# A routed expert layer on one core: accumulated rows fetched two steps earlier, with more row buffers and a smaller descriptor memory for GpSimd's transfers

## The chip, the cores and the metric

The kernel runs on one core of a Trainium2 chip. The core has five engines with instruction queues of their own: TensorE (PE in the profile; its weight loads are listed as PEld), VectorE (DVE), ScalarE (ACT), GpSimd (POOL) and SyncE (SP), and 16 DMA engines that move data. The metric is the device time of one execution in microseconds, lower is better. The kernel before takes 320.92 us, the median of three runs (320.69 to 323.11).

## The reference

The input x is 8 × 256 tokens of 512 numbers in f32. Two gated blocks follow one another, each added to its own input:

```python
x = x + jnp.tanh(g_xattn[0]) * _L0_xattn_ref(_layernorm(x), ctx_2048, mask_BxS2_bk0)
x = x + jnp.tanh(g_ffn[0]) * _L0_ffn_ref(_layernorm(x), w_router, w_gate, w_up, w_down)

# attention: few of the 256 context rows of each batch are unmasked
scores = einsum('bsd,bmd->bsm', h, ctx) / sqrt(512)
out = einsum('bsm,bmd->bsd', softmax(where(mask, scores, -1e30)), ctx)

# experts: 8 of them, inner width 192, each token uses its best 2
probs = softmax(xt @ w_router.T)
top_v, top_i = top_k(probs, 2); top_v = top_v / sum(top_v)
out = einsum('tei,ehi,te->th', silu(g) * u, w_down, comb)
```

g and u are the token's products with the expert's w_gate and w_up; comb holds the two weights of a token at its two experts. What matters here is the second block: 2048 tokens, each computed by two experts, the two results added.

## The kernel before

**First stage (to about 99 us).** Attention runs over 16 tiles of 128 tokens. It also works out each token's two experts and sorts the tokens into lists per expert, one set of lists for first choices and one for second choices. Each list is padded to tiles of 128 rows, so a tile belongs to one expert. The centred tokens, with their scales and weights behind them, are written to a table xc_d in the chip's main memory (rows of 576 numbers); ids holds, per tile, which row each of its 128 places takes. A padded place has the number of an extra row. In this stage the row buffers (tag "row", 512 numbers in each of 128 partitions) hold centred contexts, squares (L398) and the one-hot rows at_row and at_col (L440) that build the tables.

**Expert stage.** The function run (L700) goes through 38 tiles: 19 of first choices, then 19 of second choices. A tile takes these functions:

- gather (L632): GpSimd's indirect transfer fetches 128 rows by ids. With "xg" it reads xc_d into one of eight places in xall (the ring); with "acc" it reads acc_d into a row buffer.
- turn (L648): PE transposes the tile (pt_g), ACT copies it out (xT_g).
- gate_up (L651): PE multiplies with the expert's gate and up weights (pgu), ACT and DVE form h.
- flip (L669): PE transposes h (pht), DVE copies it (hT).
- down (L678): PE multiplies with the down weights (py), ACT scales the result into a row buffer y (L686). For a first-choice tile DVE adds the token's residual (L688) and GpSimd scatters y to acc_d (L645). For a second-choice tile y waits.
- add (L693): a second-choice tile's y gets the accumulated rows acc added on DVE (L695) and GpSimd scatters it to the output (L645).

Each scatter is followed on GpSimd by a one-element memset (spacer, L461). The scatters to one table are declared independent of one another; a gather from acc_d depends on all scatters to it.

**What sets the order.** The whole stage is inside a manual schedule: every engine executes its instructions in the order in which the code issues them. At step s, run issues in turn: xg for tile s + 4 (AHEAD), gate_up of tile s, flip of s - 1, turn of s + 2, down of s - 2, then acc for tile s - 3 and add for tile s - LAG = s - 4, the last two for second-choice tiles alone. There are 38 + LAG steps. Behind the down of tile 18, the last first-choice tile (step 20), a branch (L726, L728) goes round extra tiles, which this input does not need; the same branch closes the stage. GpSimd's indirect transfers thus stand in one queue: xg, acc and out of each step, in that order.

Row buffers come in a ring of 7, shared by y and acc; a buffer is written again once its last reader is done. The memory in which GpSimd writes the descriptors of its transfers lies in the core's working memory too; the program's call at L769 names no size for it, which gives 16384 bytes per partition.

Of the kernel before, what the change touches and what calls it, by code (L numbers as in the profile page):

```python
# [31 lines left out]
Q2 = NQ  # L32
# [14 lines left out]
def gated_xattn_moe(ctx: ExitStack, tc: tile.TileContext, x, xT, ctxn, ctxT, mask, maskT, g_x, g_f, wr, wgu, wd, out):  # L47
    nc = tc.nc
# [4 lines left out]
    wk = ctx.enter_context(tc.tile_pool(name="work", bufs=1))  # L53
# [7 lines left out]
    def make(pool, size, tag, bufs, shape, name):  # L61
        if not apart:
            return pool.tile(shape, FP, tag=tag, bufs=bufs, name=name)
        key = "bank" if tag == "ps" else name.split("_")[0]
        if key not in apart[0]:
            apart[0][key] = pool.tile([P, size], FP, tag=tag, bufs=bufs, name=name)
        n = math.prod(shape[1:])
        v = apart[0][key][0:shape[0], 0:n]
        return v if len(shape) == 2 else v.rearrange("p (a b) -> p a b", a=shape[1])

    def row(shape, name):
        return make(wk, 512, "row", 7, shape, name)

    def half(shape, name):
        return make(wk, 256, "half", 8, shape, name)
# [68 lines left out]
    acc_d = dr.tile([T + 1, D], FP, name="acc_d")  # L144
# [112 lines left out]
    def m_centre(p):  # L257

        g = row([P, D], f"cc_{p}")
        nc.scalar.activation(g, cns[p], AF.Identity, bias=KEEP["cmv", p][:, 0:1], scale=-1.0)  # L260
        KEEP["cc", p] = g
# [21 lines left out]
    def long_way():  # L283
# [8 lines left out]
        for b in range(B):  # L292
# [7 lines left out]
            for i in range(b * TT, (b + 1) * TT):  # L300
                nc.vector.bn_stats(one["l_st"], xs[i])
                nc.vector.bn_aggr(mv, one["l_st"])
                nc.vector.tensor_scalar(mv[:, 1:2], mv[:, 1:2], EPS, None, ALU.add)
                nc.gpsimd.tensor_tensor(rs, mv[:, 1:2], expo, ALU.pow)
                xa = row([P, D], "lx")
                nc.vector.tensor_scalar(xa, xs[i], mv[:, 0:1], rs, ALU.subtract, ALU.mult)
                xaT = turned(xa, "l")
# [15 lines left out]
                for c in range(MC):  # L323
                    nc.tensor.matmul(pav, lhsT=prT[:, c, :], rhs=cn[:, c, :], start=(c == 0), stop=(c == MC - 1))
                more = row([P, D], "lm")
                nc.vector.tensor_scalar(more, pav, den, None, ALU.mult)
                nc.vector.tensor_add(xs[i], xs[i], more)
# [367 lines left out]
        nc.vector.tensor_add(y, y, a)  # L695
        scatter(out, q, y, "out")

    AHEAD, LAG = 4, 4

    def run(qs, side=None, after=None):  # L700

        n = len(qs)

        def at(f, s, *more):
            if 0 <= s < n:
                f(*more[:1], qs[s], *more[1:]) if more else f(qs[s])
        for s in range(min(AHEAD, n)):
            at(gather, s, xc_d, "xg")
        for s in range(min(2, n)):
            at(turn, s)  # L710
        for s in range(n + LAG):
            at(gather, s + AHEAD, xc_d, "xg")
            at(gate_up, s)
            at(flip, s - 1)
            at(turn, s + 2)
            at(down, s - 2)
            if side and s >= 2 and s - 2 < n and qs[s - 2] == after:
                side()
            if 0 <= s - 3 < n and qs[s - 3] >= Q2:
                at(gather, s - 3, acc_d, "acc")  # L720
            if 0 <= s - LAG < n and qs[s - LAG] >= Q2:
                at(add, s - LAG)

# [18 lines left out]
    with tc.manual_schedule(engines={PE, DVE, ACT, POOL, SP}):  # L742
        run([*range(N0), *range(Q2, Q2 + N0)], lambda: more_tiles(0), N0 - 1)
        more_tiles(1)
# [31 lines left out]
```

## Time and profile before

| | us |
|---|---|
| median of three runs | 320.92 |
| the profiled execution | 320.94 |
| its span, first to last instruction | 319.2 |
| PE busy | 261.9 (82%) |
| POOL busy | 150.8 (47%) |
| DVE busy | 131.7 (41%) |
| ACT busy | 115.4 (36%) |
| POOL, xg gathers (38) | 37.0 busy, 975 ns each; 3.5 us to landing |
| POOL, acc gathers (19) | 18.2 busy, 957 ns each; 3.6 us to landing |
| POOL, scatters to acc_d (19) | 19.3 busy, 1015 ns each; 2.8 us to landing |
| POOL, scatters to out (19) | 19.3 busy, 1015 ns each; 2.8 us to landing |
| DVE, adds of acc (19) | 12.9 busy, 680 ns each |

The profile is of one execution. Busy time counts an engine's instructions; the time of an indirect transfer on POOL is the time that GpSimd is occupied with it, while its data land later, and the landing is counted from the issue. A line of the profile's order of time has the start, the length, the engine, the source line, the operation with output and inputs, and in brackets how long the engine was idle before it and what ended that. The mean granted clock of PE is 0.944 of full speed.

### The profile page before, as it was taken

The numbers are of one execution on the slowest core, as the hardware profiler recorded it, in microseconds if no ns is written. First come the engines' busy times: TensorE is split into PE (matmuls) and PEld (weight loads), VectorE is DVE, ScalarE is ACT, GpSimd is POOL, SyncE is SP. The second block draws the span as 40 slices with busy tenths as digits, with TensorE's granted clock in tenths as the row PEclk, the third lists the DMA queues.
The fourth block names the chain that finished last, engine by engine and source line by source line (L and its number), as shares of the span: only waits on it lengthen the run. The fifth ranks groups of instructions, "written<-read, shape, count | busy, mean of one in ns | idle before, by whom it ended". The sixth has DMA issues, their size and how long they took to land. (4 is left out here: it accounts for less than half of the span.)

```text
span 319.2 us, 4026 instructions
## 1 busy us (share of the span) xinstructions
PE 261.9 (82%) x1100; PEld 165.7 (52%) x1100; DVE 131.7 (41%) x449; ACT 115.4 (36%) x275; POOL 150.8 (47%) x238
## 2 busy tenths in 40 slices
PE   3377897979850999999999999989999999999100
PEld 3265676767630566555555565545556555555000
DVE  3329988886760024333443334422242332425100
ACT  1123677767640233333332333323233332422100
POOL 4328855665654404253353443524656566444610
PEclk9999999999975699999999999999999999999855
DMA  5699769697214602233323324316355554423510
GB/s 165 222 349 310 249 231 341 221 367 280 94 75 130 203 3 90 88 106 105 113 93 109 103 99 137 105 57 177 129 150 160 166 173 148 139 76 100 161 61 0
DMA packets 16077, 48.55 MB, mean 152 GB/s; under 512 B 3181, under 2 KB 3181, under 8 KB 16048
## 3 DMA queue, kind: packets, MB, share of 16 engines
q0 software_dynamic: 7984, 25.64, 25.7%
q1 hardware_dynamic: 5888, 17.85, 16.3%
q10 hardware_dynamic: 2176, 4.72, 3.8%
q8 instruction: 13, 0.21, 0.3%
q14 instruction: 16, 0.13, 0.1%
HBM read 35.08 MB, written 14.68 MB: 156 GB/s over the span
## 5 line engine op out<-in xcount | busy, mean ns | idle before, releaser
L658 PE MATMUL pgu<-wgu_sb,xT_g 128*128 x304 | 106.1, 492 | 0.9 <-ACTq L728 0.9
L658 PEld LDWEIGHTS pgu<-wgu_sb,xT_g 128*128 128x128 f32 x304 | 58.1, 192 | 49.4 <-issue 17.9
L682 PE MATMUL py<-wd_sb,hT 96*128 x152 | 71.4, 592 | 0.0
L664 DVE SCALAR_TENSOR_TENSOR th<-th,pgu 128x192 f32<-128x192 f32 x38 | 13.5, 354 | 103.0 <-ACT th L663 103.0
L645 POOL DMA_INDIRECT acc_d<-y,ids x19 | 19.3, 1015 | 60.3 <-DVE y L688 57.6
L640 POOL DMA_INDIRECT xall<-xc_d,ids x38 | 37.0, 975 | 17.9 <-DMA xc_d<-xr 5.0
L663 ACT ACTIVATE th<-pgu,xall 128x192 f32<-128x192 f32 x38 | 16.0, 421 | 75.2 <-PE pgu L658 75.2
L686 ACT ACTIVATE y<-py,xall 128x512 f32<-128x512 f32 x38 | 26.1, 687 | 42.1 <-PE py L682 40.0
L682 PEld LDWEIGHTS py<-wd_sb,hT 96*128 96x128 f32 x152 | 25.9, 190 | 18.8 <-issue 18.8
L445 POOL TENSOR_SCALAR ac<-cols,low,idt 128x128 f32<-128x128 f32 x32 | 27.5, 869 | 14.8 <-DVE low L439 13.8
L645 POOL DMA_INDIRECT out<-y,ids x19 | 19.3, 1015 | 31.6 <-DVE y L695 29.3
L181 PE MATMUL pt_g<-ident,xall 128*128 128x128 f32 x152 | 23.8, 281 | 8.8 <-issue 8.3
L183 ACT COPY xT_g<-pt_g 128x512 f32<-128x512 f32 x38 | 22.3, 586 | 19.6 <-PE pt_g L181 19.6
L688 DVE SCALAR_TENSOR_TENSOR y<-xall,y 128x512 f32<-128x512 f32 x19 | 14.3, 752 | 28.7 <-ACT y L686 28.7
L181 PEld LDWEIGHTS pt_g<-ident,xall 128*128 128x128 f32 x152 | 18.3, 144 | 9.6 <-issue 8.5
L354 PE MATMUL psc<-cT,xT 128*128 128x137 f32 x128 | 19.1, 293 | 3.9 <-ACT cT L268 3.2
L640 POOL DMA_INDIRECT acc<-acc_d,ids x19 | 18.2, 957 | 5.4 <-issue 5.4
L354 PEld LDWEIGHTS psc<-cT,xT 128*128 128x128 f32 x128 | 17.0, 199 | 5.0 <-ACT cT L268 3.9
L384 PE MATMUL pav<-cn,prT 128*128 128x512 f32 x32 | 16.4, 594 | 0.0
L695 DVE TENSOR_TENSOR y<-y,acc 128x512 f32<-128x512 f32 x19 | 12.9, 680 | 8.4 <-DMA acc<-acc_d,ids 8.2
L666 DVE SCALAR_TENSOR_TENSOR h<-th,xall,pgu 128x192 f32<-128x192 f32 x38 | 15.8, 415 | 1.4
L673 PEld LDWEIGHTS pht<-ident,h 128*96 128x96 f32 x76 | 9.6, 126 | 12.7 <-issue 7.5
(149 smaller groups left out, 294.7 us busy)
## 6 DMA issues: line engine op xcount, KB each, us to landing
wgu_sb<-wgu SPq DMA_DIRECT2D x8, 768.0 KB, 7.9
xc_d<-xr ACTq DMA_DIRECT2D x8, 576.0 KB, 4.0
xT<-xT SPq DMA_DIRECT2D x8, 512.0 KB, 5.0
wd_sb<-wd SPq DMA_DIRECT2D x8, 384.0 KB, 7.1
xall<-x SPq DMA_DIRECT2D x1, 2048.0 KB, 13.3
xall<-x SPq DMA_DIRECT2D x2, 512.0 KB, 4.1
xall<-x SPq DMA_DIRECT2D x1, 1024.0 KB, 9.2
xall<-xc_d,ids POOLq DMA_INDIRECT x38, 3.5
```

Of the source, the lines that this page charges most:

```text
L181: nc.tensor.transpose(pt[:, c, :], src[:, c * P:(c + 1) * P], ident)
L183: nc.scalar.copy(dst, pt)
L354: nc.tensor.matmul(both, lhsT=xTs[b][:, c, t * P:(t + 1) * P], rhs=cTs[p % 2][:, c, :], start=(c == 0), stop=(c == HC - 1))
L384: nc.tensor.matmul(pav, lhsT=prT, rhs=cns[p], start=True, stop=True)
L445: nc.gpsimd.tensor_scalar(at_col[:, n, :], cols, low[:, n:n + 1], idt[:, i:i + 1], ALU.is_equal, ALU.mult)
L640: nc.gpsimd.indirect_dma_start(out=g, out_offset=None, in_=src[:, :], in_offset=bass.IndirectOffsetOnAxis(ap=ids[:, q:q + 1], axis=0))
L645: free(nc.gpsimd.indirect_dma_start(out=dst, out_offset=bass.IndirectOffsetOnAxis(ap=ids[:, q:q + 1], axis=0), in_=z, in_offset=None, boun ...
L658: nc.tensor.matmul(pgu, lhsT=xgT[:, c, :], rhs=wgu_sb[:, bass.ds(v * GU + c * 2 * I, 2 * I)], start=(c == 0), stop=(c == HC - 1))
L663: nc.scalar.activation(th, pgu[:, 0:I], AF.Tanh, scale=xg[:, RS:RS + 1])
L666: nc.vector.scalar_tensor_tensor(h, th, xg[:, R2:R2 + 1], pgu[:, I:2 * I], ALU.mult, ALU.mult)
L682: nc.tensor.matmul(py, lhsT=hT[:, k, :], rhs=wd_sb[:, bass.ds(v * DN + k * D, D)], start=(k == 0), stop=(k == 1))
L686: nc.scalar.activation(y, py, AF.Copy, scale=xg[:, c:c + 1])
```

## The change

The order in run is changed: acc is gathered for tile s - 1 at step s instead of tile s - 3, and the add comes at step s for tile s - 3 instead of s - 4 (LAG 3), so that there are 41 steps instead of 42. The row buffers become 12 instead of 7. The descriptor memory of GpSimd's transfers becomes 2048 bytes per partition instead of 16384.

```diff
     def row(shape, name):
-        return make(wk, 512, "row", 7, shape, name)
+        return make(wk, 512, "row", 12, shape, name)
...
-    AHEAD, LAG = 4, 4
+    AHEAD, LAG = 4, 3
...
-            if 0 <= s - 3 < n and qs[s - 3] >= Q2:
-                at(gather, s - 3, acc_d, "acc")
+            if 0 <= s - 1 < n and qs[s - 1] >= Q2:
+                at(gather, s - 1, acc_d, "acc")
             if 0 <= s - LAG < n and qs[s - LAG] >= Q2:
                 at(add, s - LAG)
...
-    nc = bacc.Bacc("TRN2", target_bir_lowering=False, num_devices=1)
+    nc = bacc.Bacc("TRN2", target_bir_lowering=False, num_devices=1, dynamic_dma_scratch_size=2048)
```

In the compiled order of the instructions, GpSimd's queue behind the branch was xg 25, xg 26, acc 19, xg 27, acc 20, out 19; it is now acc 19, xg 25, acc 20, xg 26, acc 21, out 19. At the end its last six transfers were out 34, acc 36, out 35, acc 37, out 36, out 37; they are now acc 36, out 34, acc 37, out 35, out 36, out 37. DVE's adds each stand one step earlier; PE's order is the same.

## The prediction

> **What bounds the kernel now.** I read the busy times over the span first, then busy time by stretches, then the chain of waits, and last the order of time at the end and between the two passes.
>
> ```profile
> PE   3377897979850999999999999989999999999100
> ...
> PEclk9999999999975699999999999999999999999855
> ...
> POOL acc L640 5%; POOL out L645 4%; POOL xall L640 3%; PE pgu L658 2%; PE py L682 1%; POOL spacer L461 1%; PE pt_g L181 0%; ACT xT_g L183 0%; PE pht L673 0%; POOLq L726 0%; POOLq L645 0%; POOLq L640 0%; ACTq L183 0%
> ```
>
> One slice is 8 us. From 136 to 296 us PE is full; its last three slices are empty. The chain of what ended last nevertheless runs through POOL's acc, out and xall transfers. Both can hold at once: POOL's last piece is the end of the kernel, while PE sets the pace before it. The stretches settle which:
>
> ```profile
> 225.00:287.00 62.00, 62.00 (x226) 35.91 (x225) 20.59 (x49) 20.76 (x37) 35.42 (x49) 1.00 0.48 146
> 287.00:306.00 19.00, 9.39 (x27) 4.30 (x25) 6.32 (x13) 3.17 (x5) 10.34 (x16) 0.85 0.39 127
> 306.00:319.00 13.00, 0.00 (x0) 0.00 (x0) 0.00 (x0) 0.00 (x0) 0.00 (x0) 0.50 0.04 16
> ```
>
> Columns: length, then PE, weight load, DVE, ACT, POOL. In the second pass PE is busy 62.00 of 62.00 us at clock 1.00: there, POOL's waits cost nothing. In the 19 us after it PE works 9.39 us, and this stretch is where an earlier gather can pay. Its POOL and DVE instructions, in order of time (start, length, releaser):
>
> ```profile
> 290.10 0.97 POOL L640 DMA_INDIRECT acc<-acc_d,ids  x1 [0.25 <-issue]
> ...
> 293.30 1.01 POOL L645 DMA_INDIRECT out<-y,ids  x1 [2.23 <-DVE y L695]
> ...
> 294.62 0.97 POOL L640 DMA_INDIRECT acc<-acc_d,ids  x1 [0.25 <-issue]
> ...
> 295.90 1.02 POOL L645 DMA_INDIRECT out<-y,ids  x1 [0.30 <-issue]
> 296.43 0.69 ACT L686 ACTIVATE y<-py,xall 128x512 f32<-128x512 f32 x1 [1.03 <-PE py L682]
> ...
> 297.22 0.98 POOL L640 DMA_INDIRECT acc<-acc_d,ids  x1 [0.24 <-issue]
> 298.12 0.69 DVE L695 TENSOR_TENSOR y<-y,acc 128x512 f32<-128x512 f32 x1 [3.89 <-DMA acc<-acc_d,ids]
> ...
> 300.41 0.98 POOL L640 DMA_INDIRECT acc<-acc_d,ids  x1 [0.25 <-issue]
> ...
> 303.86 0.69 DVE L695 TENSOR_TENSOR y<-y,acc 128x512 f32<-128x512 f32 x1 [2.43 <-DMA acc<-acc_d,ids]
> 304.83 1.02 POOL L645 DMA_INDIRECT out<-y,ids  x1 [2.04 <-DVEq L728]
> ```
>
> Count the tiles of both passes 0 to 37, steps likewise. The last y (tile 37) is ready at 296.43 + 0.69 = 297.12, but its accumulated rows are asked for at 300.41, since that gather stands in step 40, behind four acc and out transfers. They land 3.45 us later, the add runs at 303.86, and the last out is issued at 304.83. So 7.7 us pass from a ready y to the last scatter, nearly all of it queue order.
>
> **acc gathered two steps earlier, add one step earlier.** The rows give the new order in the tail. Tile 35's gather takes the place of tile 33's in step 36, before this fence; tile 36's takes 290.10, tile 37's takes 294.62. DVE's adds each move up one place, into slots where the trace already has an add of the same length (step 37: 292.34; step 38: 293.54). So the out transfers at 293.30 and 295.90 keep their times and now carry tiles 34 and 35. Tile 36: y ready 295.40, add to 296.14, out behind POOL's previous transfer and spacer at 297.22. Tile 37: gather 294.62 + 3.45 = 298.1 (y is ready at 297.12), add 0.69 us to 298.8, out 0.28 us later at 299.07. Before: 304.83. Gain 304.83 - 299.07 = 5.76 us. The late one is now the landing of tile 37's gather, 1.0 us behind its y. The 13.3 us from the last spacer (305.91) to the end hold the last landing (2.2 to 4.2 us, median 2.8) and the program's close, which are unchanged and move along.
>
> Bounds: tile 37's out cannot precede 298.55 (POOL free behind tile 36's out and spacer), a gain of 6.3 us; with the longest landing of such a gather (4.9 us) it is 1.45 us later, a gain of 4.3 us.
>
> **Between the passes.** The first acc gather moves from third to first in POOL's queue behind the branch (step 20), and must wait for the last acc_d scatter.
>
> ```profile
> 209.94 1.01 POOL L645 DMA_INDIRECT acc_d<-y,ids  x1 [2.66 <-DVEq L728]
> ...
> 214.62 0.97 POOL L640 DMA_INDIRECT xall<-xc_d,ids  x1 [3.60 <-DMA acc_d<-y,ids]
> ...
> 215.89 0.95 POOL L640 DMA_INDIRECT xall<-xc_d,ids  x1 [0.30 <-issue]
> ```
>
> POOL waits for that landing already, in front of a gather that does not read acc_d: the branch's not-taken side waits for all of POOL's transfers. So the new wait is old. Queued behind the acc gather, tile 25's xg goes from 214.62 to about 215.9 and lands at 219.4; PE turns that tile at 221.9. Tile 26's goes from 215.89 to 218.4, lands at 221.9, is turned at 226.86. Cost nothing; were the first cover gone, at most the 1.27 us between two POOL transfers. Tile 19's add stands at 218.5, its rows land at 214.62 + 3.6 = 218.2.
>
> **Second pass, steady.** Each step still issues one xall, one acc and one out, and the out still waits for an add at the same place in DVE's queue. The xall at 225.67 lands 3.5 us later and is first read by PE's transposes at 236.77, so PE's 4.96 us a step stay. Cost nothing; the cover is those 7.6 us between landing and transposes.
>
> **12 row buffers.** Two rows a step in the second pass mean that a buffer comes round after six steps. Its last reader is then done for at least two steps, so no gather waits for a buffer. In the first stage the buffers carry at_row, at_col and squares; two of the eight groups of at_col instructions lose a wait on PE. The last of them (89.27) starts 0.19 us behind DVE's low (89.08), its ordinary handoff, so 0; a bound of 1.0 us gain is POOL's whole idle time put down to PE there.
>
> **Descriptor memory an eighth as large.** No row shows its filling. The trace has POOL transfers starting 1.28 us apart at the closest and gathers landing within 4.9 us: four open at once. If the chip must check an older transfer before it reuses memory, that costs δ per transfer; a gain is excluded, since the same rows are described. Bounds: 0, and 1.0 us (a transfer's whole busy time on POOL, 0.96 to 1.02). Nearest row: POOL's queue takes a semaphore event in 17 to 43 ns, so I take 0.04. Three transfers lie on the tail's path (out, acc, out): 0.1 us. By the Trainium skill (DMA: Bandwidth & Descriptors, sections Terms and The descriptor swizzle) a 128-partition transfer writes 9 descriptors of 16 bytes per engine and side, by which, as an estimate, 2048 bytes hold 128, or 14 transfers: no waiting for room; no trace here shows the filling.
>
> **Sum.** 5.76 - 0.1 = 5.7 us. The profiled run took 320.94 us (span 319.2), 0.02 above the median 320.92: 315.2 us.
>
> **Rivals.**
> Slower: δ is large. In the second pass POOL's step is 0.975 + 0.957 + 1.015 + 0.09 busy and about 0.80 of handoffs, 3.84 of 4.96 us; room 1.12 us, or 0.37 per transfer (first pass: two transfers, room 1.2 per transfer). Steps 22 to 33 issue three each: backlog 12 × (3δ - 1.12). Steps 34 to 37 issue two and win back 4 × (2.27 - 2δ), as a step of about 4.85 us holds 2.58 + 2δ. The tail adds 3δ. At δ = 1: 22.6 - 1.1 + 3 - 5.76, so +18.7 or 340 us. The gain is gone at δ = 0.6; over 0.67 it is over 1% slower. For it: wrapping has no row. Against: it needs ten times the nearest row. Chance 0.11.
>
> Serial transfers: the memory holds so little that each transfer waits for the one before to land. A first-pass step takes 2.8 + 3.5 = 6.3 us for 4.96, a second-pass one 3.5 + 3.6 + 2.8 = 9.9 us: 19 × 1.3 + 15 × 4.9 = 98, about 415 us. The Trainium skill (Perfetto Trace Analysis, DMA Instruction — SWDGE) says that the engines start early "particularly if more descriptors are generated than fit in the descriptor buffer"; by that rule a full buffer holds up GpSimd, which the trace with the large memory cannot show. Against: five gathers in a row are held to nothing but 1.28 us each, and an eighth would have to be less than two transfers. Chance 0.06.
>
> No gain: the acc gathers are earlier in the queue but the tail's end stays, by δ between 0.5 and 0.67, or because tile 37's rows land 5 us late among the outs. 318 to 324, likeliest 320.9. Against: 3.4 us landings in that same traffic. Chance 0.11.
>
> **Numbers.** Within 1% (3.2 us) this kernel can't be told from no change. Forecast 315.2, chance 0.72; its own range 313.6 (gain 6.3 and the 1.0 us of at_col) to 317.5 (landing +1.45, δ up to 0.3). To leave out under 2 in 10 the range takes in the no-gain case: 313.6 to 321.0. Faster by over 1% 0.72, same 0.11, slower 0.17.
>
> **What would show it.** Right: the last out is issued about 8.3 us, not 14.0, after the last gate-and-up matmuls end (290.80); its add released by y's or acc's landing within 1 us of the last y; PE still full to 296. Wrong: POOL's indirect transfers longer than 1.0 us or more than 0.3 us apart where nothing is waited for (δ); out waits growing step by step through the second pass; PE idle before pt_g; a tail whose adds still wait over 2 us for acc.

## The result and the profile after

The changed kernel takes 307.03 us, the median of four runs (306.57 to 308.71). The kernel before takes 321.29 us (four runs, 320.69 to 323.11). The ratio is 0.9565, with a 95% interval of 0.9517 to 0.9613. That is 14.3 us less, where 5.7 were predicted; 307.03 lies 6.6 us below the bottom of the predicted range.

The profiled execution of the changed kernel took 308.71 us, the slowest of the four, with a span of 307.0 us. Cut at three events which both profiles have, the two spans compare like this (us; "gate-up" is the pgu matmuls of L658):

| part of the span | before | after | difference |
|---|---|---|---|
| start to the first xg gather | 99.63 | 101.84 | +2.2 |
| to the end of the last gate-up | 191.17 | 191.32 | +0.1 |
| to the issue of the last out | 14.03 | 8.83 | −5.2 |
| to the end of the span | 14.38 | 5.00 | −9.4 |
| span | 319.21 | 306.98 | −12.2 |

The first row varies between executions: the change leaves that stage's order alone but for two buffer waits, and a second profile of the same changed kernel (e7 below) has 99.94 there. Why it varies was not found: four of the six profiles of the changed order with a small memory have 101.5 to 101.8, every other profile of the whole kernel 99.6 to 100.1. Without this row the profiles differ by 5.2 + 9.4 = 14.6 us, close to the 14.3 us of the medians. The third row is what was predicted. The fourth is not: it was taken as unchanged.

The busy time over the span and the chain of waits, from the page of the changed kernel:

```profile
PE   3289798888964199999999999998999999999990
...
PEclk9999999999996579999999999999999999999997
...
PE 24%; issue 3%; POOL 3%; DVE 1%; POOLq 0%; ACT 0%
PE pgu L658 13%; PE py L682 8%; PE pt_g L181 2%; POOL out L645 1%; PE pht L673 1%; POOL acc L640 1%; DVE y L695 0%; ACT th L663 0%; DVE h L666 0%; POOL spacer L461 0%; DVE th L664 0%; DVE hT L675 0%; POOLq L726 0%; POOLq L645 0%
```

One slice is 7.7 us. PE now has one empty slice at the end, where it had two and one nearly empty. The chain, which ran back through POOL's acc, out and xall transfers before, now runs through POOL for the last transfers only and then through PE's gate, up and down products: with the last gathers out of the way, PE's work is what leads to the end. The stretches of the changed kernel (length; then busy time and count of PE, weight load, DVE, ACT, POOL; then clock, DMA share, GB/s):

```profile
225.00:287.00 62.00, 62.00 (x224) 35.70 (x223) 21.75 (x52) 21.50 (x38) 35.65 (x49) 1.00 0.51 153
...
303.00:307.00 4.00, 0.00 (x0) 0.00 (x0) 0.00 (x0) 0.00 (x0) 0.04 (x1) 0.50 0.13 51
```

In the second pass PE is as full as before, 62.00 of 62.00 us at clock 1.00. The empty stretch behind the last instruction, 13 us before, is 4 us. DMA is busy 13% of those 4 us against 4% of the 13: the same last landing in a shorter time.

The tail in order of time, where the last gate-up ends at 290.40 + 2.75 = 293.15:

```profile
290.40 2.75 PE L658 MATMUL pgu<-wgu_sb,xT_g 128*128 x8
...
295.65 1.01 POOL L645 DMA_INDIRECT out<-y,ids  x1 [2.22 <-DVE y L695]
...
296.97 0.98 POOL L640 DMA_INDIRECT acc<-acc_d,ids  x1 [0.24 <-issue]
...
297.78 0.69 DVE L695 TENSOR_TENSOR y<-y,acc 128x512 f32<-128x512 f32 x1 [1.25 <-ACT y L686]
298.25 1.12 POOL L645 DMA_INDIRECT out<-y,ids  x1 [0.30 <-issue]
298.78 0.69 ACT L686 ACTIVATE y<-py,xall 128x512 f32<-128x512 f32 x1 [1.03 <-PE py L682]
...
299.67 1.02 POOL L645 DMA_INDIRECT out<-y,ids  x1 [0.24 <-issue]
...
301.01 0.69 DVE L695 TENSOR_TENSOR y<-y,acc 128x512 f32<-128x512 f32 x1 [2.54 <-DMA out<-y,ids]
301.98 0.99 POOL L645 DMA_INDIRECT out<-y,ids  x1 [1.24 <-DVE y L695]
302.95 0.09 POOL L461 MEMSET spacer<- 1x1 f32 x1
```

Tile 37's gather starts 3.82 us behind the last gate-up and its y is ready at 298.78 + 0.69, 6.32 us behind it: both to the hundredth where the prediction put them (294.62 and 297.12 against 290.80). From the gather's issue to the add that needs its rows it is 301.01 − 296.97 = 4.04 us instead of the 3.45 assumed, so the last out is issued 8.83 us behind the last gate-up, not 8.27. The view puts that wait down to an out transfer; by the trace's landing records the gather landed at 300.93, 0.08 us ahead of the add, and the out then under way (298.25) only at 301.78, so it was the rows. The tile before it no longer waits for rows: its add at 297.78 is released by y itself.

What fills the last stretch is not in any view, since semaphore and drain instructions are not counted as busy. They are in the trace's records, though. GpSimd's own, with start in us and length in ns (one of each in the first 0.6 us is left out):

```
before   11.77   198 semaphore | 212.65  1167 semaphore | 307.84  2177 semaphore
        310.05  8324 drain     | 318.59   107 drain     | 318.94    40 drain
after    11.77   197 semaphore | 215.00   447 semaphore | 304.96   337 semaphore
        305.33   811 drain     | 306.36   107 drain     | 306.70    40 drain
```

"Semaphore" is the instruction that the records name INC_SWDGE_SEM. It stands at a branch of the first stage, when GpSimd has made one transfer, at the branch between the passes, and at the close of the program, where a drain follows. Before, the last out (304.83) had landed when this instruction began at 307.84; then the two instructions took 2.18 + 8.32 = 10.5 us. After, they take 0.34 + 0.81 = 1.15 us. The difference, 9.35 us, is the whole of the fourth row.

### The profile page after: what moved, and what is told of

It reads as the page before. It is cut to its first block, busy times and chain, and to the rows that moved or that the text cites. A ratio compares the mean times of both kernels' runs of the same rounds, so it can differ in the third digit from the quotient of the medians.

```text
span 307.0 us, 4001 instructions
## 1 busy us (share of the span) xinstructions
PE 265.1 (86%) x1100; PEld 168.5 (55%) x1100; DVE 131.6 (43%) x449; ACT 115.4 (38%) x275; POOL 151.1 (49%) x238
## 5 line engine op out<-in xcount | busy, mean ns | idle before, releaser
L658 PE MATMUL pgu<-wgu_sb,xT_g 128*128 x304 | 106.2, 492 | 0.9 <-ACTq L728 0.9
L658 PEld LDWEIGHTS pgu<-wgu_sb,xT_g 128*128 128x128 f32 x304 | 58.2, 193 | 49.4 <-issue 17.9
L640 POOL DMA_INDIRECT xall<-xc_d,ids x38 | 37.1, 976 | 14.6 <-issue 6.1
L688 DVE SCALAR_TENSOR_TENSOR y<-xall,y 128x512 f32<-128x512 f32 x19 | 14.3, 751 | 28.7 <-ACT y L686 28.7
L354 PE MATMUL psc<-cT,xT 128*128 128x137 f32 x128 | 20.0, 303 | 3.9 <-ACT cT L268 3.2
L354 PEld LDWEIGHTS psc<-cT,xT 128*128 128x128 f32 x128 | 18.0, 209 | 5.2 <-ACT cT L268 3.9
L384 PE MATMUL pav<-cn,prT 128*128 128x512 f32 x32 | 17.3, 623 | 0.0
L675 DVE COPY hT<-pht 96x256 f32<-96x256 f32 x38 | 15.7, 414 | 0.0
```

The costliest lines, as they stand in the source:

```text
L354: nc.tensor.matmul(both, lhsT=xTs[b][:, c, t * P:(t + 1) * P], rhs=cTs[p % 2][:, c, :], start=(c == 0), stop=(c == HC - 1))
L384: nc.tensor.matmul(pav, lhsT=prT, rhs=cns[p], start=True, stop=True)
L640: nc.gpsimd.indirect_dma_start(out=g, out_offset=None, in_=src[:, :], in_offset=bass.IndirectOffsetOnAxis(ap=ids[:, q:q + 1], axis=0))
L658: nc.tensor.matmul(pgu, lhsT=xgT[:, c, :], rhs=wgu_sb[:, bass.ds(v * GU + c * 2 * I, 2 * I)], start=(c == 0), stop=(c == HC - 1))
```

## The experiments

Theory A, formed on these records: the close costs a fixed time for each transfer that the descriptor memory still holds. GpSimd has made 101 transfers at the end; by the theory 16384 bytes hold them all, 2048 only the latest few. The semaphore instruction gives a first slope: 198 ns with 1 transfer made, 1167 with 50 at the branch, 2177 with 101, so (1167 − 198) / 49 and (2177 − 1167) / 51, both 20 ns each. The drain would be 8324 / 101 = 82 ns each. The rivals are that the order, or the buffers, shortened the end and the memory nothing, or that the cost goes with the size of the memory, whatever it holds.

### One part at a time

**e1**, the memory alone, is the kernel before with

```diff
-    nc = bacc.Bacc("TRN2", target_bir_lowering=False, num_devices=1)
+    nc = bacc.Bacc("TRN2", target_bir_lowering=False, num_devices=1, dynamic_dma_scratch_size=2048)
```

> The kernel before with the descriptor memory at 2048 bytes and nothing else. Theory A (the close of the program grows with what the descriptor memory holds): GpSimd's last drain falls from 8.3 to about 0.8 us and the semaphore instruction ahead of it from 2.2 to 0.3 us, so the last out to the end of the span takes about 5.0 us instead of 14.4, and the time is 321.3 - 9.4 = about 312; the tail of out and acc transfers keeps its 14.0 us from the end of the last gate-and-up matmuls to the last out. Rival B (the close is shorter because the order of the last transfers changed): 321, with 14.4 us behind the last out. Rival C (the smaller memory also speeds or slows transfers in the middle): the stretch from the first xg gather to PE's end differs from 196.8 us by over 1 us.

**e2**, the order alone, is the changed kernel with the large memory; 12 row buffers don't fit beside it, so it has 7:

```diff
-        return make(wk, 512, "row", 12, shape, name)
+        return make(wk, 512, "row", 7, shape, name)
...
-    nc = bacc.Bacc("TRN2", target_bir_lowering=False, num_devices=1, dynamic_dma_scratch_size=2048)
+    nc = bacc.Bacc("TRN2", target_bir_lowering=False, num_devices=1)
```

> The changed order (acc for tile s - 1, add for s - 3) with 7 row buffers and 16384 bytes of descriptor memory, as 12 buffers do not fit beside it. Theory A: only the tail gets shorter, 14.0 to 8.8 us from the end of the last gate-and-up matmuls to the last out, the end behind it stays 14.4 us: 321.3 - 5.2 = about 316. Rival B: the close falls to 5 us, about 307. If the buffers are needed: acc gathers or y wait for a buffer and the gain is under 4 us.

**e3** is the changed kernel with 7 row buffers (the first of these two edits alone).

> The changed kernel with 7 row buffers instead of 12. If the buffers carry nothing: 307.0 within 1 us, the same tail of 8.8 us. If they are what lets the gathers run early: out of acc gathers that wait for a buffer, a longer tail, up to 312.

**e4** is the kernel before with half the memory, `dynamic_dma_scratch_size=8192`.

> The kernel before with 8192 bytes of descriptor memory. Theory A by what is held: the memory holds some 56 of the 101 transfers (each taking 9 of 512 places), at 82 ns each in the drain (8324 ns over 101) and 20 ns in the semaphore instruction: drain 4.6 us, semaphore instruction 1.3 us, time 321.3 - 4.6 = 316.7. Theory A by size alone: half of 8.3 and 2.2 us, time 316.1. Rival B: 321.

All four were timed beside the kernel before (median 321.24, seven runs). The last two columns are from their profiles.

| kernel | median, us | ratio (95%) | last gate-up to last out | last out to end |
|---|---|---|---|---|
| before | 321.24 | | 14.03 | 14.38 |
| e1, memory alone | 311.77 | 0.9696 (0.9646 to 0.9747) | 13.74 | 5.09 |
| e2, order alone | 316.19 | 0.9821 (0.9768 to 0.9874) | 9.14 | 14.35 |
| e3, changed, 7 buffers | 307.43 | 0.9545 (0.9491 to 0.9599) | 9.12 | 5.02 |
| e4, half the memory | 315.33 | 0.9804 (0.9751 to 0.9857) | 13.76 | 9.20 |

The two parts are separate and add up: 9.5 us for the memory and 5.05 for the order make 14.5, where 14.3 were to be explained. The tails of e1 and e2, in order of time, show each with one half of the change:

```profile
300.69 0.98 POOL L640 DMA_INDIRECT acc<-acc_d,ids  x1 [0.24 <-issue]
...
303.98 0.69 DVE L695 TENSOR_TENSOR y<-y,acc 128x512 f32<-128x512 f32 x1 [1.91 <-DMA acc<-acc_d,ids]
304.95 1.02 POOL L645 DMA_INDIRECT out<-y,ids  x1 [1.21 <-DVE y L695]
...
305.94 0.09 POOL L461 MEMSET spacer<- 1x1 f32 x1
```

This is e1: the last add still waits for acc, and the last out starts at 304.95, as before (304.83). From the first xg gather to the last gate-up e1 takes 191.34 us, where before has 191.17, so the small memory doesn't slow the transfers in the middle. In its stretches (the same columns as above) the end that follows is as short as in the changed kernel:

```profile
306.00:310.00 4.00, 0.00 (x0) 0.00 (x0) 0.00 (x0) 0.00 (x0) 0.03 (x1) 0.50 0.13 51
```

And e2, its tail and then its stretches:

```profile
295.33 0.97 POOL L640 DMA_INDIRECT acc<-acc_d,ids  x1 [0.25 <-issue]
...
299.67 0.69 DVE L695 TENSOR_TENSOR y<-y,acc 128x512 f32<-128x512 f32 x1 [2.84 <-DMA acc<-acc_d,ids]
300.64 0.99 POOL L645 DMA_INDIRECT out<-y,ids  x1 [1.54 <-DVE y L695]
301.61 0.09 POOL L461 MEMSET spacer<- 1x1 f32 x1
```

```profile
302.00:315.00 13.00, 0.00 (x0) 0.00 (x0) 0.00 (x0) 0.00 (x0) 0.00 (x0) 0.50 0.04 16
```

Its acc comes early and its last out starts at 300.64, but the 13 empty us stand behind it as before. The records of GpSimd's closing instructions follow the memory and not the order (ns):

```
              memory   semaphore   drain
before, e2     16384  2177, 2182    8324
e4              8192        1162    4159
after, e1, e3   2048    337, 342     811
```

e4 tells a size between the two ends. Its closing semaphore instruction, 1162 ns, is as long as the one with 50 transfers made at the branch (1167), so by the theory about 50 were still held. Its drain then costs 4159 / 50 = 83 ns each; a line through the two drains gives (8324 − 4159) / 51 = 82 ns each and some 0.1 us besides. The semaphore instruction of 337 ns after the change means about 8 held, by which the drain would be 0.7 us; it is 0.81. By size alone e4 would show half of 2177 and 8324 ns, and it does, so e4 doesn't decide between the two rules (and its median, 315.33, lies about 1 us below what was expected by either); the one length of 1167 ns at the branch with 16384 bytes speaks for the transfers, and the small kernels below decide it. The Trainium skill (DMA: Bandwidth & Descriptors, the section on the descriptor swizzle) counts nine descriptors per engine and side for a transfer of 1 MiB to 128 partitions; with 16 bytes for each (its section Terms) 56 transfers fit in 8192 bytes and 14 in 2048, as an estimate. The counts of about 50 and 8 that the lengths tell agree with that: they lie below those bounds. By the theory the older ones were cleared away in passing.

e3 answers for the buffers. In e3's profile, the acc gathers (count, then lowest, median and longest ns, and when), and below them the idle time in front of all 57 gathers of that line, xg and acc, and what ended it (us and count):

```profile
L640 POOL DMA_INDIRECT acc<-acc_d,ids x19: 942/946/1764, 216.2 to 296.6; - x19
...
  issue: 14.4, 42
  DMA xc_d<-xr: 5.0, 1
  ACT th L663: 3.5, 14
```

No wait for a reader of a row buffer is among them with 7, and its time, 307.43, is that of the changed kernel. The 12 buffers carry nothing.

### The cost by itself

Does the close go by the transfers held or by the bytes? And what does it cost to reuse a small memory while work goes on? Four small kernels make GpSimd gather 128 rows of x in a loop, with 8 buffers, and store the first 16:

```python
for i in range(GATHERS):
    k = i % NT
    g = wk.tile([P, D], FP, tag="g", name=f"g_{i}")
    nc.gpsimd.indirect_dma_start(out=g, out_offset=None, in_=x[:, :],
                                 in_offset=bass.IndirectOffsetOnAxis(ap=ids[:, k:k + 1], axis=0))
    if i < NT:
        nc.sync.dma_start(out=out[k * P:(k + 1) * P, :], in_=g)
```

m1 has 32 gathers and 16384 bytes, m2 96 and 16384, m3 96 and 2048, m4 32 and 32768.

> A small kernel alone: 32 gathers of 128 rows of x by GpSimd, the first 16 stored to the output; attention and experts are left out. Descriptor memory 16384 bytes. If the drain grows with the transfers that were made and not yet cleared away (82 ns each): 32 x 82 = 2.6 us. If it grows with the size of the memory: 8.3 us as in the kernel before.

> The same with 96 gathers in 16384 bytes. By transfers: 96 x 82 = 7.9 us. By size: 8.3 us, the same as with 32 gathers.

> 96 gathers in 2048 bytes, of which the memory holds 14 at a time. By transfers held: at most 14 x 82 = 1.1 us. By size: 1.0 us. Clearing transfers away in between should show in the gathers: none over 1.2 us and a spacing as with 16384 bytes if it is cheap, 0.1 us more a gather if it costs what the drain costs.

> 32 gathers in 32768 bytes. By transfers: 2.6 us as with 16384 bytes. By size: 16.6 us.

| | time, us | span | start of the last gather | from there to the end |
|---|---|---|---|---|
| m1, 32 of 16384 | 51.21 | 49.1 | 43.37 | 5.69 |
| m4, 32 of 32768 | 51.01 | 48.9 | 43.32 | 5.54 |
| m2, 96 of 16384 | 135.77 | 134.0 | 124.36 | 9.64 |
| m3, 96 of 2048 | 130.60 | 128.8 | 123.88 | 4.95 |

m1 and m4 agree to 0.15 us with memories of different size, and neither shows the 8.3 or 16.6 us that the size alone would give, so the bytes don't count. 64 more gathers in the same memory make the close 3.95 us longer (m2 against m1), and with the small memory those 96 close within 4.95 us. In m2 the drain ends 7.9 us after GpSimd has issued its last gather: 96 × 82 ns. One expectation can't be read as it was put: the 2.6 us for 32 transfers do not show in m1. There the last gather takes 3.56 us to land and the drain ends 1.35 us behind the landing, less than 2.6, so part of its work seems to lie beside the landing. All these transfers are of 128 rows: whether the close goes by the transfer or by its descriptors is not shown. The numbers are of one execution each.

In m2 and m3 the gathers themselves (line; busy time in us and mean ns; idle time before them and what ended it), and their last:

```profile
L27 POOL DMA_INDIRECT g<-x,ids x96 | 90.8, 946 | 33.5 <-issue 26.5 <-DMA out<-g 6.4 <-DVE ids L23 0.6
...
124.36 0.95 POOL L27 DMA_INDIRECT g<-x,ids  x1 [0.30 <-issue]
```

```profile
L27 POOL DMA_INDIRECT g<-x,ids x96 | 90.9, 947 | 33.0 <-issue 29.1 <-DMA out<-g 2.5 <-DMA g<-x,ids 0.8
...
123.88 0.95 POOL L27 DMA_INDIRECT g<-x,ids  x1 [0.30 <-issue]
```

946 and 947 ns each, 0.30 us apart, and the last one at the same time to 0.5 us, although the small memory is written over many times: clearing in passing costs nothing that can be seen. Together with e1 this settles the prediction's δ, and its rival of serial transfers too. The Trainium skill (Perfetto Trace Analysis, DMA Instruction — SWDGE) speaks of more descriptors than fit in the buffer; with 2048 bytes no gather in m3 was held up by it. With 1024, in e6 and e8 below, a few single transfers took 1.2 to 1.7 us, as single ones did with more memory.

### What is late next

In the changed kernel tile 37's add waits 1.5 us for its rows (y at 299.47, add at 301.01). **e5** asks for them one step earlier still, and two tiles at the first step behind the branch:

```diff
-            if 0 <= s - 1 < n and qs[s - 1] >= Q2:
-                at(gather, s - 1, acc_d, "acc")
+            for i in (s - 1, s) if s == N0 + 1 else (s,) if s > N0 + 1 else ():
+                at(gather, i, acc_d, "acc")
```

> The changed kernel with acc gathered for tile s at step s (tiles 19 and 20 together at step 20, the first step behind the last scatter to acc_d). Theory A: in the changed kernel the last add still waits for the landing of tile 37's rows, asked for in step 38 behind out 34. A step earlier it waits for y alone, out 35, 36 and 37 follow one another as POOL and DVE allow: last out about 1.5 us earlier, 7.3 us after the last gate-and-up matmuls end instead of 8.8, close still 5.0 us, about 305.5. If POOL's own queue of outs is what holds the end: 307.

**e6** is e5 with `dynamic_dma_scratch_size=1024`, and **e7** is the changed kernel once more, for its spread.

> The same with 1024 bytes of descriptor memory, room for 7 transfers of 9 places. Theory A: at most 7 transfers are held at the end instead of 6 to 7 now, so drain and semaphore instruction stay at 0.8 and 0.3 us or fall by at most 0.5 us together: 305.0 to 305.5. If waiting for room begins to cost: gaps of more than 0.3 us between POOL's transfers where four stand in a row (first gathers, behind the branch), and over 305.5.

> The changed kernel once more beside the two, unchanged: 307.0 within 1 us, drain 0.8 us, last out 8.8 us after the end of the last gate-and-up matmuls. First xg gather between 99.6 and 101.9 us, if the 2.2 us by which it came later in its first profile are the spread of the first stage between executions.

| kernel | median, us | ratio (95%) | first xg to end of last gate-up | to last out | to end |
|---|---|---|---|---|---|
| e5 | 307.55 | 0.9542 (0.9503 to 0.9580) | 192.28 | 7.32 | 5.28 |
| e6 | 306.80 | 0.9530 (0.9496 to 0.9564) | 191.96 | 7.56 | 4.88 |
| e7 | 308.09 | 0.9574 (0.9537 to 0.9611) | 191.44 | 9.08 | 4.99 |

The tail is 1.5 to 1.8 us shorter than e7's, as expected; the 305.5 us expected of e5, and 305.0 to 305.5 of e6, were missed. In these profiles part of it is lost earlier: from the first xg gather to the last gate-up e5 and e6 take 192.28 and 191.96 us, where the profiles of before and after have 191.17 and 191.32. In e5 PE waits 0.7 us for h. The three intervals overlap, so none of this is a gain that can be told. In e6 the closing instructions are 297 and 647 ns, about 6 transfers held.

The lost time might have come from the second gather at the branch. **e8** therefore is e6 with the step made four tiles later, in the full second pass:

```diff
-            for i in (s - 1, s) if s == N0 + 1 else (s,) if s > N0 + 1 else ():
+            for i in (s - 1,) if N0 < s < N0 + 5 else (s - 1, s) if s == N0 + 5 else (s,) if s > N0 + 5 else ():
```

> As the run with 1024 bytes and acc for tile s at step s, but the shift from s - 1 to s is made at step 24, where two acc gathers stand together, and no longer at step 20 behind the branch, so that tile 25's xg is not put back. If the second acc gather behind the branch is what cost 0.6 to 0.9 us between the first xg gather and the last gate-and-up matmuls (192.0 and 192.3 us there, 191.1 to 191.4 in the others): 191.3 again, no wait of PE for h of 0.7 us, last out 7.4 us after these matmuls, about 306. If it is the earlier acc in itself: 192 again, 306.8.

It takes 305.47 us (305.02 to 307.96), ratio 0.9471 (0.9434 to 0.9507): the fastest of all and below both expected times, its interval just clear of the changed kernel's (from 0.9517), though not of that of e6. The tail is 7.56 us and the close 4.88, as in e6. In the tail in order of time:

```profile
299.33 0.69 ACT L686 ACTIVATE y<-py,xall 128x512 f32<-128x512 f32 x1 [1.03 <-PE py L682]
300.05 0.69 DVE L695 TENSOR_TENSOR y<-y,acc 128x512 f32<-128x512 f32 x1 [1.03 <-issue]
...
301.26 0.98 POOL L645 DMA_INDIRECT out<-y,ids  x1 [0.58 <-DVEq L728]
```

The last add follows its y by 0.03 us: the rows are there, and nothing is left to gain from an earlier gather. What was expected of the stretch to the last gate-up didn't come: it is 192.21 us, as long as in e5. PE's waits behind the branch (mean us, count, sum) are

```profile
PE pht L673 <- DVE h L666: 0.9, 1, 0.9
PE pgu L658 <- ACTq L728: 0.8, 1, 0.8
```

The second is the branch itself, the only one that the changed kernel has. The first is e5's loss again, without a second gather at the branch. In front of it lie pauses of 3 to 5 us on ACT (before the instructions at 227.7 and 232.6 in e5, 230.8 in e6, 228.1 and 231.7 in e8), for which no reason was found in the trace: in e5 the copy of xT_g (227.69) starts 3.0 us behind the end of its transposes. The view puts that wait down to PE's py, which the copy does not read and which ended 1.3 us before it.

The trace itself gives a hint of where they are from. It keeps a record of every landing on a semaphore, and in these profiles many are missing, most of them behind 220 us:

```
landing records: before, after, e1 to e4   2255 or 2256 each
                 e7 1843 | e6 1705 | e5 1655 | e8 1589
```

Such pauses behind 220 us are in the four incomplete traces and in none of the six complete ones (all ten have one of 3.0 to 3.1 us at the branch), and e7, which has one of 3.2 us at 226.1, is the changed kernel, whose first trace has none. So the order alone does not make them. But e5, e6 and e8 have more or longer ones than e7, and e1 to e4 were run on another chip than e5 to e8, so neither the order's share nor the chip's is ruled out. e8's profiled execution, 307.96 us, is 2.1 us above the highest of its six others (305.02 to 305.86), while those of e6 and e7 (306.40 and 307.19) lie below their medians. Whether the recording held the engines up, or something else disturbed both, was not tried. The loss in the stretch before the tail is not put down to the kernels; their medians stand.

## Why the prediction was wrong

**The close: the step that failed.** The prediction said: "The 13.3 us from the last spacer (305.91) to the end hold the last landing (2.2 to 4.2 us, median 2.8) and the program's close, which are unchanged and move along." 13.3 less 2.8 left 10.5 us to which no row was put, and they were taken as a constant. They are GpSimd's semaphore instruction and drain, 2.18 + 8.32 us, and they grow with the transfers that the descriptor memory holds. With 2048 bytes they are 1.15 us. e1 shows it by itself: that one edit takes 9.5 us off, 9.3 of it behind the last out in the profiles.

**The descriptor memory.** "A gain is excluded, since the same rows are described" is the same error in the other place: the bounds looked at what a transfer costs when it is made, and not at what it costs while it stays. δ itself was right to be small. 0.04 us was taken; GpSimd's gathers are 946 and 947 ns each with the large and the small memory in m2 and m3, and all indirect transfers of the kernel take 989 ns before and 991 after, on average.

**The tail.** 5.76 us predicted, 5.2 in the profile, 5.05 from e2's median. The order came out as worked through; the one term that was off is the landing of tile 37's rows, 4.04 us instead of 3.45. With it the last add came 1.5 us behind its y, where the prediction gave "within 1 us" as a sign of being right.

**Between the passes.** Right: it cost nothing. The acc gather goes first behind the branch in the changed kernel:

```profile
212.30 1.01 POOL L645 DMA_INDIRECT acc_d<-y,ids  x1 [2.66 <-DVEq L728]
213.27 0.09 POOL L461 MEMSET spacer<- 1x1 f32 x1
...
216.52 0.97 POOL L640 DMA_INDIRECT acc<-acc_d,ids  x1 [3.16 <-issue]
...
217.80 0.95 POOL L640 DMA_INDIRECT xall<-xc_d,ids  x1 [0.30 <-issue]
```

The gap behind the last scatter is 3.16 us, in front of an acc gather now and of an xg gather then (3.60), and the xg stands 1.28 us behind it. PE has no wait there but the 0.9 us of the branch. The semaphore instruction at the branch also fell, from 1167 to 447 ns, and that paid nothing: 191.17 us before and 191.32 after from the first xg to the last gate-up.

**The second pass and the buffers.** Right: PE full in both profiles, and e3 with 7 buffers no slower.

**The rivals.** A large δ and serial transfers are refuted by m3 and by the page of the changed kernel. "No gain" is refuted by e2. The case that came true, a gain from the memory, was on no list.

**Two readings.** Of PE's last three slices, which the prediction calls empty, the first shows one tenth. POOL's transfers start 1.25 us apart at the closest before the change, not 1.28. Neither changes the sum.

## What to carry to other kernels

A kernel's end has work in it that busy time doesn't count: when the profile shows many empty microseconds behind the last landing, find the instructions that fill them in the trace's records before calling them constant. Where GpSimd makes many transfers, try a descriptor memory that holds only a few of them: here 2048 bytes instead of 16384 took 9.5 us off by itself, cost the transfers nothing that could be seen, and left 14 KiB per partition free. And a load that an in-order queue holds behind stores paid here in the last few steps only; while PE was full, its place didn't count.

## What the runs showed of the hardware

- At the close GpSimd spends about 20 ns (semaphore instruction) and 80 ns (drain) on each transfer that its descriptor memory still holds: 10.5 us with 101 held, 5.3 with some 50, 1.15 with about 8, 0.94 with about 6 (the last three counts are worked out from the length of the semaphore instruction).
- It goes by transfers and not by the size of the memory (m1, m2 and m4), and those cleared in passing cost nothing visible (m2 and m3).
- Single transfers of 1.3 to 1.8 us on GpSimd turn up in some profiles (1302 ns in e2 with 16384 bytes, 1764 in e3 with 2048, 1659 in e6 with 1024), so with every size of memory; that they cost time was not seen in the medians.
- Profiles can be incomplete and disturbed at once: four that lost 400 to 670 of 2256 landing records have pauses of 3 to 5 us on ACT behind 220 us that no complete one has. Which causes which is open.
